# A graph-attention kernel on one core: batch 0's self features as seven block products, and the loads of batch 1 in pieces

## The chip, the core and the metric

The kernel runs on one core of a Trainium2 chip. A core has a matrix engine (TensorE, PE in the profile; its weight loads are listed apart as PEld), three engines for elementwise work (VectorE, DVE; ScalarE, ACT; GpSimd, POOL) and a queue engine (SyncE, SP) that issues nearly all DMAs here. Engines run their own instruction lists in order and wait for each other through semaphores. The metric is the device time of one execution in microseconds (us); lower is better.

## The reference

A graph-attention layer over B = 16 batches of N = 512 nodes with F = 512 features; only the first NG = 20 nodes of a batch are attended to, there are 16 heads of 32, two directions d, and 11 edge labels.

```python
row_zero = v.sum(-1) == 0
q_exp = where(row_zero[..., None], 0.0, q[:, None, :])
self_feat = concatenate([v, q_exp], -1) @ W_self.T + b_self      # (B, N, 512)
output = self_feat
for d in range(2):
    A = (adj if d == 0 else swapaxes(adj, 1, 2))[:, :, :20, :]   # (B, N, 20, 11)
    cond, vb = A.sum(-1), A @ w_bias + b_bias
    kv = self_feat[:, :20]
    aff = where(cond[:, :, None] > 0, q_d(self_feat) . k_d(kv) / sqrt(32), -9e15) + vb[:, :, None]
    output += einsum(softmax(aff) over the 20 nodes, kv, Wout[d]) + bout[d]
return v + relu(output)
```

The part that matters most here is `self_feat`: for each batch a 512 x 512 by 512 x 512 product in fp32, plus a query term where the node's row is not all zero.

## The kernel before

Everything is held with features on the 128 partitions (four chunks of 128) and nodes along the free dimension. There is a setup, and then a loop over 16 batches; each batch has four tiles (`nt` = 0 to 3) of 128 nodes. The order of the instructions on every engine is the order in which the program writes them (`manual_schedule`); nothing reorders them.

**Setup.** Weights are loaded; the features of the 20 attended nodes of all batches (`kvn`, `kvT`) and their keys (`khD`) are computed. Keys are then multiplied by the query weights, so that scores can be taken from `self_feat` directly. This runs in 22 bursts (`keys`): a burst is 16 small matmuls into two PSUM pairs, which ScalarE (L683) and VectorE (L685) empty into the stage tiles `st`; finished stages go out by DMA, to `g0` (batch 0, kept in SBUF), `g1_d` (batch 1) and `g_d` (the others), both in HBM. A burst uses both PSUM pairs, so the next can begin only when both are emptied; between two bursts TensorE does something else, by the list `plan`: one entry per burst from the fifth (n = 4) on, each letter one step. `v` and `w` are the products that make the values (`values`, results to `vw_d` in HBM), `c` the bias scores (`bias_scores`), `n` the flags for rows that are zero (`row_flags`), `s` a sixteenth of a part of batch 0's self features (`self_step`, L205). VectorE adds the query term to a finished part (`self_copy`, L218). POOL, in the same bursts, sums rows (`row_sums`), makes sums and differences of the blocks of W_self (`weight_sums`) and multiplies the masks of batch 0 (`mask_mul`, `mask_count`, `mask_sum`, `mask_spread`).

**Self features.** For batches 1 to 15 the product is done by blocks: x and W_self are cut in two by two blocks, and seven products of 246 columns (`product`, L282) of sums of blocks (`x_sum` on POOL, `weight_sums`) stand for the eight plain ones; `partial` (L289) and `joined` (L299) on VectorE read them out of PSUM and add the query term. The 20 attended nodes are copied from `kvn` (`new_self`). For batch 0 the plain products are used, in four parts `(f, h)` (output half f, node half h): three in the setup, the fourth in batch 0 between the scores of its first and second tile (`self_feat(0, 1, 1)`).

**A tile.** `scores` (L356, 128 matmul records), into one of two PSUM pairs; `weigh` on VectorE adds the masks (`full_add` on POOL makes them from `cq` and the spread masks `both`) and subtracts the maximum; `expo` on ScalarE; one tile later `normal` (sum and reciprocal on VectorE, multiplication on POOL, L411) and `turn` (transpose into `wt`, VectorE). In tile 2 of batch b the attention of batch b - 1 is done (`attend`, L429), from `wt` and the value blocks `vd`; `finish` adds the self features and `residual` adds x.

**Value blocks.** `vd` is read from `bd_d` in HBM (`load_values`), a block-diagonal layout for all batches. In batch 0 `bd_d` is set to zero by one DMA of 2 MB (`clear_blocks`), and then 12 DMAs copy the values of all batches from `vw_d` into it, in runs of 32 numbers (`blocks`).

**SP's queue.** All these loads are issued by SP in program order, and each waits on SP for what it needs; `behind(dma, instruction)` adds a wait for a named instruction, so that loads of steady batches go out one by one. In batch 0 of the kernel before, the keys of batch 1 are loaded in one DMA ahead of the loop, and at the start of tile 1 the masks of batch 1 (`load_adj`), `cq` (`load_cq`), the clear, and the natural rows of batch 2 (`load_xn`, for the zero flags: `row_sum` on ScalarE, `row_mask` on POOL) go out without such waits; the copies stand at the start of tile 2, `load_values(0)` at the start of tile 3.

Of the kernel before, what the change touches and what calls it, by code (L numbers as in the profile page):

```python
# [13 lines left out]
P = 128  # L14
# [4 lines left out]
def gat_kernel(  # L19
# [71 lines left out]
    adds, fulls, wts, outs, held, sf_ps, conds, prods = {}, {}, {}, [], [None] * 3, {}, {}, {}  # L91
    sums, parts, us, done = {}, {}, {}, {}
# [57 lines left out]
    def blocks():  # L150

        bb = bd_d.rearrange("c b r e i g -> (c b) r e i g")
        vv = vw_d.rearrange("d c (b m) (e g) -> d (c b) m e g", m=NG, e=HL)
        for e in range(HL):
            for i in range(2):
                j = (e * S) // 32 + i
                for d in range(2):
                    lo = max(e * S + d * NG, 32 * j)
                    hi = min(e * S + (d + 1) * NG, 32 * j + 32)
                    if lo < hi:  # L160
                        m, r = lo - e * S - d * NG, lo - 32 * j
                        nc.sync.dma_start(bb[:, r : r + hi - lo, e, i], vv[d, :, m : m + hi - lo, e])
# [31 lines left out]
    def self_feat(b, f, h, parts=((0, range(C)), (1, range(C)))):  # L194


        lo, hi = max(NG, h * N // 2), (h + 1) * N // 2
        for i, ks in parts:
            if (i, ks[0]) == (0, 0):
                if (f, h) == (0, 0):  # L200
                    new_self(b)
                held[0] = bank(f"ps_sf{b}_{f}{h}", 3 if (f, h) == (1, 1) else None)
            for k in ks:
                for a in range(HL):
                    nc.tensor.matmul(  # L205
                        held[0][bass.ts(a, R), i * N // 2 : i * N // 2 + hi - lo],
                        ws_v[:, k, bass.ds((2 * f + i) * P + a * R, R)], xs[b][:, k, lo:hi],
                        start=(k == 0), stop=(k == C - 1),
                    )
            if (i, ks[-1]) == (1, C - 1):  # L210
                sf_ps[b, f, h] = held[0]

    def self_copy(b, f, h):

        lo, hi = max(NG, h * N // 2), (h + 1) * N // 2
        ps = sf_ps.pop((b, f, h))
        for i in range(2):
            nc.vector.scalar_tensor_tensor(  # L218
                sfs[b][:, 2 * f + i, lo:hi], nzs[b][:, lo:hi], qw[:, 2 * f + i, b : b + 1],
                ps[:, i * N // 2 : i * N // 2 + hi - lo], ALU.mult, ALU.add,  # L220
            )

# [15 lines left out]
    def x_sum(b, n):  # L238

        t = sums[b, n] = xsum.tile([P, 2, HN], F32, tag=f"t{n}", name=f"t{b}_{n}")  # L240
# [8 lines left out]
    def product(b, n):  # L249
# [11 lines left out]
        if n == 1:  # L261
            parts[b, "a"] = [bank(f"ps_a{b}_{i}", i) for i in range(2)]
        if n == 2:
            parts[b, "d"] = bank(f"ps_d{b}", 2)
        if n == 5:
            parts[b, "c"] = bank(f"ps_c{b}", 3)
# [30 lines left out]
    def joined(b, n, key, f, l):  # L297

        done["joined"] = nc.vector.tensor_add(  # L299
            block(b, f, l), parts[b, key][:, : 2 * HN].rearrange("p (i n) -> p i n", i=2), us.pop((b, n))  # L300
# [30 lines left out]
    def mask_spread(b, h, quarters=range(4)):  # L331

        add = conds[b, h]
        for a in quarters:
            for g in range(HL):
                r = bass.ts(g, R)
                nc.scalar.copy(adds[b, h][bass.ts(a, R), :, g], add[r].rearrange("p (t m) -> p t m", t=2))  # L337
# [29 lines left out]
    def weigh(b, nt, ps, between=None):  # L367

        f = softmax_view(fulls.pop((b, nt)))
        nc.vector.tensor_add(  # L370
# [81 lines left out]
    with tc.tile_pool(name="setup", bufs=1) as sp, tc.tile_pool(name="ps_acc", bufs=4, space=PSUM) as acc["pool"]:  # L452
# [157 lines left out]
        with tc.tile_pool(name="setup_g", bufs=4) as sg:  # L610
# [451 lines left out]
```

## Time and profile before

| | |
|---|---|
| median of 3 runs | 587.73 us (587.0 to 588.74) |
| the profiled execution's own time | 589.14 us |
| its span (first to last instruction) | 587.3 us |
| TensorE busy | 575.0 us (98%) |
| VectorE, ScalarE, POOL busy | 84%, 67%, 65% |
| granted TensorE clock | 0.995 |
| HBM traffic | 82.30 MB read, 40.24 MB written |

The profile's page lists busy times, the chain of work that ended last, the costliest groups of instructions and the DMAs; other views give an engine's instructions in order of time, who waited for whom, and busy times by stretches. In a row of a timeline the first number is the start in us from the span's start, the second the time in us until the last instruction of the row ends; `x32` counts instructions; `a<-b` is output and inputs; a bracket tells how long the engine was idle before and what ended that. Rows with SPq are DMAs being issued, and their time is that of issuing, not of the transfer. One fp32 matmul of the program leaves two matmul records. A busy TensorE is a list of matmuls without gaps; it is not TensorE at its peak.

### The profile page before, as it was taken

To read this page: it belongs to the slowest core of one execution; us is meant where nothing else is said; L and a number is where in the kernel's file an instruction comes from. 1 tells how busy PE (TensorE), PEld (TensorE's weight loads), DVE (VectorE), ACT (ScalarE), POOL (GpSimd) and SP (SyncE) were. 2 spreads that over 40 slices of the span, in tenths; PEclk is the share of its full clock that TensorE was granted. 3 is DMA by queue.
4 is the path that set the end of the run, shared out by engine and by line. 5 is a ranking of instruction groups with operands and counts; after the bars stand their busy time and mean duration, and the time that the engine had idled before them with its cause. 6 is when DMAs were issued, how large, how long until landed. Compare 5 with 4: busy or idle time off the path is not lost.

```text
span 587.3 us, 30302 instructions
## 1 busy us (share of the span) xinstructions
PE 575.0 (98%) x13180; PEld 436.8 (74%) x13180; DVE 491.2 (84%) x785; ACT 395.5 (67%) x1162; POOL 384.3 (65%) x351
## 2 busy tenths in 40 slices
PE   9999999999999999999999999999999999999993
PEld 6654547887778787877778787787878878787881
DVE  1485565889898989899999999998989898989895
ACT  1334534686877777878686868686877868776761
POOL 2406663548677685858586867776868686777774
PEclk9999999999999999999999999999999999999998
DMA  8999899857766675757676767675666766664403
GB/s 312 387 400 314 330 376 333 256 110 209 231 179 188 188 211 169 216 172 214 173 201 180 217 169 210 175 210 167 198 196 188 210 187 182 210 171 136 121 31 127
DMA packets 103221, 124.14 MB, mean 211 GB/s; under 512 B 21713, under 2 KB 71921, under 8 KB 101041
## 3 DMA queue, kind: packets, MB, share of 16 engines
q1 hardware_dynamic: 101840, 120.32, 66.3%
q8 instruction: 104, 1.70, 1.2%
q0 software_dynamic: 672, 1.36, 1.0%
q10 hardware_dynamic: 576, 0.53, 0.3%
q14 instruction: 29, 0.23, 0.1%
HBM read 82.30 MB, written 40.24 MB: 209 GB/s over the span
## 4 chain that ended last, share of the span: by engine, by line
PE 94%; DVE 3%; DMA 1%; issue 1%; ACT 0%; POOL 0%; SPq 0%; DVEq 0%; POOLq 0%; ACTq 0%
PE ps_s L356 44%; PE ps_a L282 17%; PE ps_c L282 9%; PE ps_o L429 6%; PE ps_d L282 4%; PE ps_v L643 3%; PE ps_k L580 3%; PE ps_sf L205 2%; DMA ws_q<-in_wsT 1%; PE ps_kv L531 1%; DVE o L438 0%; PE ps_nz L189 0%; DVE wt L418 0%; DVE ps_s L374 0%; DVE sm L409 0%
## 5 line engine op out<-in xcount | busy, mean ns | idle before, releaser
L356 PEld LDWEIGHTS ps_s<-g,sf 128*32 128x32 f32 x8192 | 263.3, 110 | 20.1 <-issue 12.2
L356 PE MATMUL ps_s<-g,sf 128*32 128x152 f32 x8192 | 276.7, 293 | 0.5 <-ACT st L683 0.5
L337 ACT COPY both<-add 32x80 f32<-32x80 f32 x512 | 130.9, 256 | 53.6 <-DVE add L328 47.6
L411 POOL TENSOR_TENSOR s<-s,sm 128x640 f32<-128x640 f32 x63 | 80.3, 1275 | 95.5 <-DVE sm L410 54.7
L344 POOL TENSOR_TENSOR full<-cq,both 128x640 f32<-128x640 f32 x64 | 100.2, 1565 | 28.5 <-issue 22.6
L317 ACT ACTIVATE prod<-adj,wb_sb 128x80 f32<-128x80 int32 x330 | 112.5, 432 | 0.8 <-DMA adj<-in_adj 0.8
L383 ACT ACTIVATE s<-s 128x640 f32<-128x640 f32 x63 | 46.5, 738 | 65.6 <-DVE s L378 65.3
L443 POOL TENSOR_TENSOR o<-o,x 128x512 f32<-128x512 f32 x60 | 76.0, 1288 | 0.0
L370 DVE TENSOR_TENSOR full<-ps_s,full 128x608 f32<-128x608 f32 x63 | 48.9, 777 | 29.7 <-PE ps_s L356 24.4
L409 DVE TENSOR_REDUCE sm<-s 128x32 f32<-128x640 f32 x63 | 50.9, 807 | 9.2 <-ACT s L383 8.9
L282 PE MATMUL ps_a<-t,ws_s 128*32 128x246 f32 x960 | 55.4, 370 | 0.0
L374 DVE TENSOR_REDUCE ps_s<-full 128x32 f32<-128x640 f32 x63 | 52.2, 828 | 2.2
L418 DVE STREAM_TRANSPOSE wt<-s 128x640 f32<-128x640 f32 x63 | 52.8, 839 | 0.1
L378 DVE TENSOR_TENSOR s<-full,ps_s 128x640 f32<-128x640 f32 x63 | 51.5, 818 | 1.1
L282 PEld LDWEIGHTS ps_a<-t,ws_s 128*32 128x32 f32 x960 | 31.5, 110 | 16.1
L328 DVE TENSOR_REDUCE add<-prod 128x80 f32<-128x960 f32 x32 | 36.8, 1150 | 6.1 <-ACT prod L317 4.3
L247 POOL TENSOR_TENSOR t<-x 128x492 f32<-128x492 f32 x30 | 34.4, 1148 | 10.2 <-DVE full L370 5.3
L429 PE MATMUL ps_o<-wt,vd 32*32 32x512 f32 (+5 forms) x816 | 37.8, 578 | 2.3 <-DVE wt L403 2.0
L440 ACT ACTIVATE o<-o,bo 128x512 f32<-128x512 f32 x60 | 38.3, 711 | 0.6 <-POOL biased L888 0.6
L438 DVE TENSOR_TENSOR o<-ps_o,sf 128x512 f32<-128x512 f32 x60 | 36.7, 668 | 0.0
L289 DVE SCALAR_TENSOR_TENSOR u<-nz,qw,ps_a 128x246 f32<-128x246 f32 x90 | 36.6, 449 | 0.0
L247 POOL TENSOR_TENSOR t<-x,t 128x492 f32<-128x492 f32 x30 | 34.4, 1147 | 1.9 <-DMA x<-in_xT 0.7
(238 smaller groups left out, 719.6 us busy)
## 6 DMA issues: line engine op xcount, KB each, us to landing
g_d<-st SPq DMA_DIRECT2D x16, 1064.0 KB, 5.8
g<-g_d SPq DMA_DIRECT2D x56, 304.0 KB, 3.6
out_T<-o SPq DMA_DIRECT2D x60, 256.0 KB, 3.5
x<-in_xT SPq DMA_DIRECT2D x56, 256.0 KB, 3.3
xn<-in_xn SPq DMA_DIRECT2D x52, 256.0 KB, 3.2
adj<-in_adj SPq DMA_DIRECT2D x56, 220.0 KB, 3.3
nz<-nz_d SPq DMA_DIRECT2D x14, 256.0 KB, 4.3
wk<-in_wkT SPq DMA_DIRECT2D x2, 1024.0 KB, 7.6
```

The costliest lines, as they stand in the source:

```text
L247: done["xsum"] = nc.gpsimd.tensor_sub(t, one, two)
L282: nc.tensor.matmul(to, lhs, x[:, k], start=start, stop=stop, skip_group_check=n != 2)
L317: nc.scalar.activation(p[:, :, l], a[:, :, l], AF.Identity, scale=wb_sb[:, l : l + 1])
L337: nc.scalar.copy(adds[b, h][bass.ts(a, R), :, g], add[r].rearrange("p (t m) -> p t m", t=2))
L344: done["full"] = nc.gpsimd.tensor_add(f, cqs[b].unsqueeze(1).to_broadcast(shape), adds[b, nt // 2][:, nt % 2].unsqueeze(2).to_broadcast(sh ...
L356: nc.tensor.matmul(bank[bass.ts(a, R), bass.ts(j, WD // HL)], sfs[b][:, k, bass.ds(nt * P + (2 * g + j) * R, R)], keys[:, k, a], start=(k ...
L374: nc.vector.tensor_reduce(mx, f, AX.X, ALU.max)
L378: done["weigh"] = nc.vector.tensor_sub(s, f, mx.unsqueeze(3).to_broadcast(full))
L411: done["normal"] = nc.gpsimd.tensor_mul(s, s, sm.unsqueeze(3).to_broadcast(full))
L418: nc.vector.transpose(wts[b][:, nt], s.rearrange("p a h m -> p (a h m)"))
L429: nc.tensor.matmul(banks[a][bass.ds(at // 2 * DH, n * DH)].rearrange("p (t n) -> p t n", n=32), vd[r, bass.ds(at * DH, n * DH)], wt[r, :, ...
L443: nc.gpsimd.tensor_add(o[:, c], o[:, c], xs[b][:, c])
```

## The change

Batch 0 gets its self features by the same seven block products as the others. They are steps `p` of the setup's plan, one per burst, in the last seven bursts; each is followed by its `partial` or `joined` on VectorE. For that `weight_sums` and the row sums of batch 1 move to burst 9, `new_self(0)` and the four block sums of batch 0 to burst 11; the block sums lie in a tile of the pool of the self features. The `v`, `c`, `w` and `n` steps are dealt out anew over the earlier bursts. The fourth part between batch 0's first two tiles of scores goes, with its `self_copy`. In all batches `partial` now writes straight into the self features and `joined` adds in place, without a tile of its own, and `new_self(b + 1)` stands in tile 2 in place of tile 3.

In batch 0 the loads of SP's queue are cut: `bd_d` is cleared in eight DMAs of 256 KB, batch 1's masks go out in four halves, its keys in four pieces, batch 2's natural rows in four pieces. Most wait for a named instruction of batch 0. The first three tiles order them so: two mask halves, clears 0 and 1 (tile 0); clears 2 and 3, `cq`, keys 0, clears 4 to 7 (tile 1); keys 1, two mask halves, and the 12 copies with keys 2 and 3 and the four pieces of natural rows among them (tile 2). Batch 2's x follows; `load_values(0)` moves from tile 3 of batch 0 to tile 0 of batch 1, behind `joined`. `row_sum(2)` on ScalarE moves from tile 3 of batch 0 to tile 0 of batch 1, behind the second mask product, and `row_mask(2)` behind `full_add(1, 1)`.

```diff
-    def clear_blocks(zero):
-        nc.sync.dma_start(
-            bd_d.rearrange("c b r e i g -> (c b r) (e i g)").rearrange("(n p) w -> p n w", p=P),
-            zero.unsqueeze(1).to_broadcast([P, C * B * 32 // P, HL * 2 * DH]),
-        )
+    def clear_blocks(zero, n, ins):
+        half = bd_d[n // 2, n % 2 * (B // 2) : (n % 2 + 1) * (B // 2)]
+        behind(nc.sync.dma_start(
+            half.rearrange("b r e i g -> (b r) (e i g)").rearrange("(n p) w -> p n w", p=P),
+            zero.unsqueeze(1).to_broadcast([P, B * 16 // P, HL * 2 * DH]),
+        ), ins)
...
-                        nc.sync.dma_start(bb[:, r : r + hi - lo, e, i], vv[d, :, m : m + hi - lo, e])
+                        copies.append((bb[:, r : r + hi - lo, e, i], vv[d, :, m : m + hi - lo, e]))
+        for n, (to, of) in enumerate(copies):
+            nc.sync.dma_start(to, of)
+            if n in (2, 5):
+                load_keys(1, range(n // 3 + 2, n // 3 + 3))
+            if n in (7, 8, 9, 10):
+                load_xn(2, (n - 7) // 2, None, slice((n - 7) % 2, (n - 7) % 2 + 1))
...
-    def partial(b, n, f, l, to=None):
-        if to is None:
-            to = us[b, n] = xsum.tile([P, 2, HN], F32, tag=f"u{n}", name=f"u{b}_{n}")
+    def partial(b, f, l):
+        to = block(b, f, l)
...
-            def self_step(b, f, h, i, k):
-                self_feat(b, f, h, ((i, (k,)),))
-                if (i, k) == (1, C - 1):
-                    self_copy(b, f, h)
+            def block_product(n):
+                product(0, n)
+                f, args = {
+                    1: (partial, (0, 0, 0)), 2: (joined, (0, "d", 0, 0)), 6: (partial, (0, 0, 1)),
+                    7: (partial, (0, 1, 1)), 5: (joined, (0, "c", 1, 1)), 4: (partial, (0, 1, 0)),
+                    3: (joined, (0, "c", 0, 1)),
+                }[n]
+                f(*args)
...
+                "p": [(block_product, (n,)) for n in (1, 2, 6, 7, 5, 4, 3)],
...
-            plan = "bvv vv vv ccw vv ns ssss sssw vv vv ssss ssss vv vv nww ssss ssss".split()
+            plan = "bvv vvc vvc vvn vv vvw vv vv w w wn p p p p p p p".split()
...
+                if n == 9:
+                    row_sums(1)
+                    weight_sums()
                 if n == 11:
-                    row_sums(1)
-                if n == 13:
-                    weight_sums()
+                    new_self(0)
+                    for i in range(1, 5):
+                        x_sum(0, i)
...
-        load_keys(1)
...
                 if b == 0 and nt == 1:
-                    load_adj(1, 0)
-                    load_cq(1)
-                    clear_blocks(zero)
-                    load_adj(1, 1)
-                    load_xn(2, 0)
-                    load_xn(2, 1)
-                if b == 0 and nt == 2:
-                    blocks()
-                if nt == 2 and last or nt == 3 and b == 0:
+                    clear_blocks(zero, 2, done["xsum"])
+                if nt == 2 and last:
                     load_values(b)
...
+                        if b == 1:
+                            for j in range(4):
+                                row_sum(2, j)
                         product(b, 4)
...
-                        if b > 1:
-                            load_values(b - 1, done["joined"])
+                        load_values(b - 1, done["joined"])
...
+                    if b == 0:
+                        clear_blocks(zero, 3, done["sum"])
+                        load_cq(1)
...
-                    if b == 0:
-                        self_feat(0, 1, 1)
...
+                    if b == 0:
+                        load_keys(1, range(1), done["mixed"])
+                        clear_blocks(zero, 4, done["normal"])
...
+                    if b == 0:
+                        clear_blocks(zero, 7, done["full"])
...
+                    if b == 0:
+                        load_keys(1, range(1, 2), done["sum"])
+                        load_adj(1, 1, done["normal"], slice(0, 1))
+                        load_adj(1, 1, None, slice(1, 2))
+                        blocks()
```

More of the change, by code (lines that the diff above doesn't have):

```diff
@@ L191, in row_flags @@
         nc.vector.tensor_scalar(nzs[b], ps[:, :N], 0.0, None, ALU.not_equal)
[L194 to L221, printed above, removed]
     def weight_sums():
@@ L912, in gat_kernel @@
                         product(b + 1, 2)
[L913 removed]
+                        new_self(b + 1)
+                    s = weigh(b, nt, pair, (lambda: partial(b + 1, 0, 0)) if more else None)
                     expo(s)
```

65 lines of the change are left out of this document (38 added, 27 removed).

## The prediction, made before the changed kernel was run

> **What bounds the kernel now.** I read the chain that ended last first, then TensorE's waits, then the two places that the diff touches (the bursts at the end of the setup, and SP's queue in batch 0), each on the engines' timelines.
>
> ```profile
> PE 94%; DVE 3%; DMA 1%; issue 1%; ACT 0%; POOL 0%; SPq 0%; DVEq 0%; POOLq 0%; ACTq 0%
> ```
> ```profile
> PE ps_s L356 <- ACT st L683: 0.5, 1, 0.5
> ```
> The first row is the chain that ended last, by engine: TensorE (PE) carries 94% of the span. The second is TensorE's wait ahead of the very first scores; hardly any other wait of its matmuls exists. So whatever shortens TensorE's list of matmuls counts, and whatever makes TensorE wait in batches 0 and 1 counts as much. The matmuls themselves, in the chain in order of time (start, us, what, matmul records):
>
> ```profile
> 58.06 1.73 PE ps_sf L205 x32
> ...
> 85.45 1.86 PE ps_sf L205 x32
> ...
> 91.15 4.34 PE ps_s L356 x128
> 95.49 3.45 PE ps_sf L205 x64
> ...
> 111.41 1.66 PE ps_a L282 x32
> ```
> L205 is batch 0's old self_feat: a half of a group of 236 columns takes 1.73, of 256 columns 1.86; three groups (two of 236, one of 256) are in the setup, the fourth, 3.45, stands between batch 0's first and second scores. The first scores run from 91.15 to 95.49; I call their end E. A block product (L282, 246 columns, 32 records) takes 1.66 in the loop.
>
> Now SP's queue, which issues all DMAs of batch 0 in order (start, us until the last is issued):
>
> ```profile
> 108.46 11.54 SPq L162 DMA_DIRECT2D bd_d<-vw_d  x12
> 124.38 3.12 SPq L139 DMA_DIRECT2D vd<-bd_d  x4
> 127.55 1.84 SPq L105 DMA_DIRECT2D x<-in_xT  x4
> ```
> The 12 copies into the value blocks are issued in 11.54 us, until 120.00. The read of the value blocks (vd, four DMAs) reads what they write, so it starts only at 124.38, 4.4 after the last copy's issue: this is the landing of the last copy. The attention of batch 0, which needs vd, runs on TensorE here:
>
> ```profile
> 132.06 2.24 PE L429 MATMUL ps_o<-wt,vd 32*32 32x512 f32 x48
> 134.23 4.34 PE L356 MATMUL ps_s<-g,sf 128*32 128x152 f32 x128
> 138.39 1.84 PE L282 MATMUL ps_a<-x,ws_v 128*32 128x246 f32 x32
> ```
> It starts at 132.06. How much earlier vd was there is told by its landings:
>
> ```profile
> DMA to landing us min/median/max: 1.7/3.2/3.4
> ```
> The last of the four is issued at about 127.1 (124.38 + 3.12 less its own 0.4) and is down 1.7 later, at 128.8: 4.4 after the first one's issue, and 3.3 before TensorE wanted it. That 3.3 is the room which the change can use up in SP's queue before TensorE stands.
>
> **The change part by part.**
>
> TensorE's work. Removed from the setup: 4 x 1.73 + 2 x 1.86 = 10.6. Added there: seven block products. In the setup a filler between two bursts costs more than the same work in the loop (a half of 256 columns 1.86 there, 3.45 / 2 = 1.73 in the loop), so I put 246 columns between 1.73 and 1.86: 1.80, seven are 12.6. Bounds: 1.66 (11.6) and 1.86 (13.0). Setup: +2.0. Removed from batch 0: -3.45.
>
> Fillers and evictions. Between two bursts of key products TensorE does a filler, and the next burst needs the PSUM pair that ScalarE and VectorE (DVE) empty.
>
> ```profile
> 43.16 1.98 PE L643 MATMUL ps_v<-wo_sb,kvT 128*128 128x512 f32 x4
> ...
> 56.59 0.78 PE L668 MATMUL ps_g(1, 3, 1, 0, 2)0_552<-khD,wq_sb 32*128 32x304 f32 x4
> ...
> 57.99 1.80 PE L205 MATMUL ps_sf<-x,ws_v 128*32 128x236 f32 x32
> 59.72 0.40 PE L668 MATMUL ps_g(2, 0, 0, 1, 2)0_594<-khD,wq_sb 32*128 32x152 f32 x2
> ...
> 60.70 1.40 PE L205 MATMUL ps_sf<-x,ws_v 128*32 128x236 f32 x24
> ...
> 82.53 1.94 PE L643 MATMUL ps_v<-wo_sb,kvT 128*64 128x512 f32 x8
> ```
> ```profile
> 43.32 1.17 DVE L685 TENSOR_SCALAR st<-ps_g(0, 3, 1, 1, 2)1_410 128x304 f32<-128x304 f32 x2 [0.52 <-PE ps_g(0, 3, 1, 1, 2)1_410 L668]
> ...
> 76.99 1.06 DVE L322 TENSOR_REDUCE cond<-adj 128x80 f32<-128x880 int32 x1
> ...
> 109.14 0.84 DVE L289 SCALAR_TENSOR_TENSOR u<-nz,qw,ps_a 128x246 f32<-128x246 f32 x2
> ```
> In the burst before 43.16 the eviction starts 0.16 after the filler and takes 1.17: a filler shorter than 1.33 makes TensorE wait. The new plan has two bursts followed by a lone w step; two w steps together take 1.94 (82.53), so one takes 0.97: two waits of about 0.37. Old waits that go: the burst at 56.59 lasts until 57.99, 1.40, where the one at 59.72 lasts until 60.70, 0.98 (0.42, behind a VectorE that was late), and the 0.5 ahead of the first scores, since a product now stands between the last burst and them. VectorE's new load is two instructions per partial (0.84) and one per join, which I count at 0.84 too: 1.17 + 0.84 = 2.0 in a burst of 0.98 + 1.80 = 2.78, hidden; only where batch 0's second mask count (1.06) joins them, 3.07, does it stick out by 0.3. Sum of waits: 0.74 + 0.3 - 0.92 = +0.1; bounds -0.9 (no new wait) and +2 (0.3 at each of the seven products).
>
> POOL. Row sums, weight sums and four subtractions move ahead. The first product that uses a sum is the third, six bursts behind the subtractions' place; four POOL operations at 1.28 (the row of 640 elements below) are 5.1 against at least 5 x 2.78. Nothing on the path; if POOL were that late, each product would wait for one subtraction.
>
> So the first scores begin at 91.15 + 2.0 + 0.1 = 93.2, E moves from 95.49 to 97.6 (+2.1), and everything behind the old fourth group is 2.1 - 3.45 = -1.4 earlier: attention of batch 0 is due at 130.7.
>
> SP's queue. Clearing the value blocks becomes 8 DMAs instead of 1, batch 1's masks 4 instead of 2, its keys 4 instead of 1, batch 2's natural rows 4 instead of 2; most wait for a named instruction of batch 0, and what is queued behind such a wait waits too. The gates end with the last clear, which waits for the third full_add of batch 0, on POOL:
>
> ```profile
> 103.94 1.57 POOL L344 TENSOR_TENSOR full<-cq,both 128x640 f32<-128x640 f32 x1
> 107.87 1.28 POOL L411 TENSOR_TENSOR s<-s,sm 128x640 f32<-128x640 f32 x1 [2.36 <-DVE sm L410]
> ```
> It ended at 103.94 + 1.57 = 105.5, which is E + 10.0; nothing of it depended on the old fourth group, so with the new E it ends at 107.6, and the last clear goes out there. The first copy waits for that clear to land; 256 KB take
>
> ```profile
> out_T<-o SPq DMA_DIRECT2D x60, 256.0 KB, 3.5
> ```
> 3.5, so copies start at 111.1. Bounds: the two mask halves in front of them wait for the next POOL row (normal, 1.28, till 108.9) and cost two plain issues (0.46, a quarter of the 1.84 for x): not before 109.8; and 114.6 with twice the landing. Among the 12 copies now stand 6 plain DMAs (two of keys, four of rows). I charge 6 x 0.46 = 2.8; lower bound 0 (the copies' queue has room), upper 6 x 0.96 = 5.8 (the copies' own pace). Copies issued by 111.1 + 11.5 + 2.8 = 125.4, landed 4.4 later at 129.8. Batch 2's x, which was behind vd, now goes ahead of it, but in the time of that landing. vd needs 4.4 again: 134.2. TensorE wants it at 130.7 and stands 3.5. Queued behind the attention are the next tile's scores and everything after, so the stall goes into the time in full.
>
> Late next. Keys of batch 1: the third piece is issued after three copies, the fourth after six, about 111.1 + 6 x 0.96 + 0.9 = 117.8, landing (3.5) 121.3. The second half of batch 1's first scores is due, counted back from 132.06 by a tile of scores (4.3), a product (1.7) and half a tile (2.2), at 123.9, less 1.4: 122.5. Hidden, by 1.2; if that cover is gone, TensorE stands here first and the attention's stall is as much shorter. Row sums of batch 2 on ScalarE now stand behind the second mask product and wait for rows that are issued among the last copies:
>
> ```profile
> 121.14 3.77 ACT L317 ACTIVATE prod<-adj,wb_sb 128x80 f32<-128x80 int32 x11
> 126.20 2.13 ACT L337 COPY both<-add 32x80 f32<-32x80 f32 x8 [1.29 <-DVE add L328]
> 129.00 0.74 ACT L383 ACTIVATE s<-s 128x640 f32<-128x640 f32 x1 [0.66 <-DVE s L378]
> ```
> The mask product (121.14, 3.77) ends at 123.5 in the new time. The fourth rows are the 17th of 18 issues, about 124.0, landing 127.5; a row sum (taken as the 0.74 of the exponential) ends 128.2, half a mask spread 2.13 later, so the exponential due at 127.6 starts at 130.3: 2.7 late. Its readers on VectorE feed the product at 138.39, so it costs between 0 and 2.7 by itself, and nothing while attention stands for 3.5 anyway. Writing partials straight into self_feat, joining in place, and the copy of the first 20 columns one tile earlier change no count of instructions in batches 1 to 15: nothing.
>
> Sum. +2.0 + 0.1 - 3.45 + 3.5 = +2.1. The profiled execution took 589.14 (span 587.3), 1.4 above the median 587.73: 591.2 on its scale, 589.8 on the median's.
>
> [...] How loaded the DMA engines were is in the view by stretches (us; busy time of PE, PEld, DVE, ACT, POOL; clock; DMA share, GB/s):
>
> ```profile
> 103.00:107.00 4.00, 4.00 (x132) 4.00 (x128) 3.68 (x5) 1.26 (x3) 2.51 (x2) 1.00 1.08 377
> 123.00:127.00 4.00, 4.00 (x123) 3.80 (x119) 3.47 (x5) 2.68 (x9) 3.25 (x4) 1.00 0.13 24
> ```
> vd's 1.7 landing falls into the quiet stretch (share 0.13), while the clear's stretch before had a share of 1.08. [...]
>
> **Rivals.**
> Landings are short, and vd is in time. In the quiet stretch a DMA landed in 1.7. With 1.7 for the last clear the copies start at their gate, 109.8; issued by 124.1, landed 125.8, vd there at 130.2, just before 130.7. Then -1.4 stays: 586.3; with products at 1.66 up to another 1.0 less. It decides at a vd that lands 3.5 sooner than I charge. For it: the queue is no longer filled at once. Against it: the last copy of before took 4.4, most of it in a stretch in which SP issued nothing else; x's two extra DMAs now fall into it.
> The queue is fuller. The rows and keys among the copies (6 x 0.96) and a slow clear (114.6): vd at 114.6 + 11.5 + 5.8 + 4.4 + 4.4 = 140.7, ten late: 596. With half of it, 593. For it: share 1.08 whenever large loads stood together before; against: with a share of 0.13 at 123 to 127 the engines had time to spare while SP waited for the last copy.
> The setup does not take seven products. VectorE's two instructions per product could set the pace of the last seven bursts: 0.3 each, +2 more: 592.
>
> **How the numbers follow.** A measurement of this kernel tells 0.3% (1.8 us) from no change. Forecast 0.42 (589.8, own range 588 to 592; about a third of it within 0.3%), short landings 0.30 (two thirds of it faster by over 0.3%, since the open ends of the products' and the waits' terms, 1.0 each, lie below its -1.4; the rest within), fuller queue 0.20, setup 0.08. Faster 0.20, same 0.25, slower 0.55. The range goes from 585.3 (short landings with cheap products) to 594.5 (half to three quarters of the fuller queue).
>
> **What the changed profile would show.** Right: in the setup 32-record products of about 1.8; first scores starting near 93.2; no L205; in SP's queue copies starting near 111 and vd issued near 130; a TensorE wait of some 3.5 ahead of the attention of batch 0, put down to vd. Wrong: the attention starting right behind scores near 130.7, or a wait at another place: keys of batch 1, row sums on ScalarE.

## The result, and the profile after

The changed kernel takes 591.14 us (median of 7 runs, 590.69 to 595.46) against 587.16 for the kernel before (7 runs, 586.28 to 588.74): a ratio of 1.0082, 95% interval 1.0065 to 1.0099. It is slower by 0.8%.

The chain that ended last, by engine, and TensorE's waits, of the changed kernel:

```profile
PE 88%; DVE 3%; SPq 3%; DMA 2%; issue 1%; POOL 1%; ACT 1%; DVEq 0%; POOLq 0%; ACTq 0%
```
```profile
PE ps_o L413 <- DMA vd<-bd_d: 4.9, 1, 4.9
```

TensorE's share of the chain fell from 94% to 88%; SP's queue (SPq) and DMAs, which were next to nothing, have 5%. The waits name the place: 4.9 in front of batch 0's attention (L413), for vd. The wait of 0.5 ahead of the first scores, which the prediction showed, is gone. The chain in order of time shows both parts of the change (start, us, what):

```profile
74.73 1.80 PE ps_a L267 x32
...
91.13 1.80 PE ps_c L267 x32
92.93 1.80 PE ps_s L340 x55
...
107.70 3.90 DMA bd_d<-zero
...
121.67 1.93 SPq L111
...
125.47 2.16 SPq L111
...
127.67 3.43 DMA bd_d<-vw_d
...
131.19 4.38 DMA vd<-bd_d
...
135.70 4.00 PE ps_o L413 x48
```

The seven products of the setup take 1.80 each, and the first scores start at 92.93. From 107.70 on the chain leaves TensorE: the last clear lands 3.90 after its issue, then come SP's issues, among them two rows of batch 2 (L111) at 1.93 and 2.16, the last copy lands 3.43 after its issue at 127.67, and the first piece of vd 4.38 after 131.19. TensorE's own timeline around it (start, us, engine, line, what; in brackets the idle time before):

```profile
126.30 4.46 PE L340 MATMUL ps_s<-g,sf 128*32 128x152 f32 x128
135.70 4.00 PE L413 MATMUL ps_o<-wt,vd 32*32 32x512 f32 x48 [4.94 <-DMA vd<-bd_d]
139.63 4.34 PE L340 MATMUL ps_s<-g,sf 128*32 128x152 f32 x128
...
167.93 2.24 PE L413 MATMUL ps_o<-wt,vd 32*32 32x512 f32 x48
```

The scores ahead of the attention end at 126.30 + 4.46 = 130.76. TensorE then stands 4.94, and the 48 records of the attention, 2.24 in the kernel before, take 4.00. The stretches between show why (us; busy time of PE, PEld, DVE, ACT, POOL; granted clock; DMA share, GB/s):

```profile
131.00:135.70 4.70, 0.00 (x0) 0.03 (x1) 1.98 (x4) 4.50 (x16) 1.93 (x3) 1.00 0.85 254
135.70:139.70 4.00, 4.00 (x52) 1.16 (x56) 2.24 (x3) 1.76 (x5) 4.00 (x4) 0.58 0.69 108
139.70:142.00 2.30, 2.30 (x76) 2.30 (x80) 2.22 (x4) 2.30 (x8) 0.38 (x1) 1.00 0.70 214
```

The granted clock is 0.58 in the 4 us after the wait, and 1.00 before and after. At full clock the attention would have ended 4.00 - 2.17 = 1.83 sooner (2.17 by the chain of a later experiment). The next scores start at 139.63 instead of 134.23, 5.4 later: -1.4 from the work that is gone, + 4.94 + 1.83. ScalarE and VectorE were late as well:

```profile
130.12 0.63 ACT L177 ACTIVATE xn<-xn 128x512 f32<-128x512 f32 x1 [0.49 <-DMA xn<-in_xn]
...
132.88 0.74 ACT L367 ACTIVATE s<-s 128x640 f32<-128x640 f32 x1
```
```profile
133.65 0.82 DVE L393 TENSOR_REDUCE sm<-s 128x32 f32<-128x640 f32 x1 [4.16 <-ACT s L367]
...
139.78 2.48 DVE L422 TENSOR_TENSOR o<-ps_o,sf 128x512 f32<-128x512 f32 x4 [1.80 <-PE ps_o L413]
```

The four row sums of batch 2 (L177) wait for their rows from 124.5 to 130.1, so the exponential behind them starts at 132.88 (it had been due at 127.6), and VectorE waits 4.16 for it. VectorE still stands 1.80 for the attention at 139.78: this lateness is covered by the stall.

One attention later, in batch 1, the two kernels stand 4.43 apart (167.93 above, and this row of the kernel before):

```profile
163.50 2.24 PE L429 MATMUL ps_o<-wt,vd 32*32 32x512 f32 x48
```

Between its two attentions the kernel before needed 31.44 (163.50 - 132.06), where a batch otherwise takes 30.48: its profiled execution lost 1.0 there, 1.5 in later batches and 1.2 behind the last attention. So the two profiled executions end only 1.7 apart (590.85 and 589.14), while the medians are 4.0 apart. In these two executions nothing more is lost once batch 1 attends; how much of the kernel before's own losses its other executions have is not shown, since only one has a profile.

### The profile page after: what moved, and what is told of

It reads as the page before. It is cut to its first block, busy times and chain, and to the rows that moved or that the text cites. A ratio compares the mean times of both kernels' runs of the same rounds, so it can differ in the third digit from the quotient of the medians.

```text
span 589.1 us, 30279 instructions
## 1 busy us (share of the span) xinstructions
PE 574.8 (98%) x13148; PEld 437.3 (74%) x13148; DVE 493.1 (84%) x788; ACT 395.5 (67%) x1162; POOL 388.6 (66%) x355
## 4 chain that ended last, share of the span: by engine, by line
PE 88%; DVE 3%; SPq 3%; DMA 2%; issue 1%; POOL 1%; ACT 1%; DVEq 0%; POOLq 0%; ACTq 0%
PE ps_s L340 40%; PE ps_a L267 17%; PE ps_c L267 9%; PE ps_o L413 6%; PE ps_d L267 4%; PE ps_k L564 3%; PE ps_v L627 3%; PE ps_kv L515 2%; SPq L166 1%; SPq L111 1%; DMA vd<-bd_d 1%; DMA bd_d<-zero 1%; DMA bd_d<-vw_d 1%; PE ps_warm L474 1%; POOL s L395 0%
## 5 line engine op out<-in xcount | busy, mean ns | idle before, releaser
L267 PE MATMUL ps_a<-t,ws_s 128*32 128x246 f32 x1024 | 59.4, 371 | 0.6 <-issue 0.6
L273 DVE SCALAR_TENSOR_TENSOR sf<-nz,qw,ps_a 128x246 f32<-128x246 f32 x128 | 51.6, 443 | 0.7 <-PE ps_a L267 0.7
L267 PEld LDWEIGHTS ps_a<-t,ws_s 128*32 128x32 f32 x1024 | 33.4, 110 | 18.5 <-POOL s L395 1.0
L413 PE MATMUL ps_o<-wt,vd 32*32 32x512 f32 (+5 forms) x816 | 38.6, 609 | 7.2 <-DMA vd<-bd_d 4.9
L232 POOL TENSOR_TENSOR t<-x 128x492 f32<-128x492 f32 x32 | 36.8, 1149 | 9.5 <-DVE full L354 6.9
L232 POOL TENSOR_TENSOR t<-x,t 128x492 f32<-128x492 f32 x32 | 36.7, 1146 | 1.3
```

What stands on the lines that cost most here:

```text
L232: done["xsum"] = nc.gpsimd.tensor_sub(t, one, two)
L267: nc.tensor.matmul(to, lhs, x[:, k], start=start, stop=stop, skip_group_check=n != 2)
L273: done["partial"] = nc.vector.scalar_tensor_tensor(to[:, i], nzs[b][:, half(l)], qw[:, 2 * f + i, b : b + 1], parts[b, "a"][i][:, :HN], AL ...
L413: nc.tensor.matmul(banks[a][bass.ds(at // 2 * DH, n * DH)].rearrange("p (t n) -> p t n", n=32), vd[r, bass.ds(at * DH, n * DH)], wt[r, :, ...
```

## The experiments

Theory A: the change pays for SP's queue. The copies start late behind gated clears and have other DMAs among them, so vd is late, and the clock falls behind the wait. Theory B: it pays for row sums that hold up ScalarE. Theory C: it pays in the setup. Every ratio is against the kernel before on the same chip in the same session, with a 95% interval. The last column is the ratio times 587.16 us; the expected times are to be held against it, since they start from the chip on which the kernel before took 587.16. (The 587.1 that e7 and e8 name for e1 is its own median, with 588.04 for the kernel before beside it.)

| kernel | ratio | interval | us at 587.16 |
|---|---|---|---|
| changed kernel | 1.0082 | 1.0065 to 1.0099 | 591.14 |
| e1 block products alone | 0.9983 | 0.9969 to 0.9998 | 586.2 |
| e2 loads alone | 1.0073 | 1.0051 to 1.0096 | 591.4 |
| e3 ten matmuls in the wait | 1.0139 | 1.0118 to 1.0160 | 595.3 |
| e12 five matmuls in the wait | 1.0085 | 1.0063 to 1.0107 | 592.2 |
| e4 scores ahead of the attention | 1.0058 | 1.0035 to 1.0082 | 590.6 |
| e5 rows early | 1.0040 | 1.0026 to 1.0054 | 589.5 |
| e6 no named waits | 0.9987 | 0.9966 to 1.0009 | 586.4 |
| e7 block products, rows behind the copies | 0.9999 | 0.9989 to 1.0008 | 587.1 |
| e11 no named waits, vd ahead of x, late row sums | 0.9997 | 0.9979 to 1.0015 | 587.0 |
| e8 block products, clear ahead of keys | 0.9997 | 0.9985 to 1.0009 | 587.0 |
| e9 block products, clear in the setup | 1.0011 | 0.9998 to 1.0023 | 587.8 |
| e10 the same, other loads spread | 1.0041 | 1.0020 to 1.0063 | 589.6 |

**e1, e2: the two halves of the change.** e1 keeps the new products and puts every load back; e2 keeps the old self_feat and takes every new load.

```diff
 e1 (against the changed kernel)
+        load_keys(1)
                 if b == 0 and nt == 1:
-                    clear_blocks(zero, 2, done["xsum"])
+                    load_adj(1, 0)
+                    load_cq(1)
+                    clear_blocks(zero)
+                    load_adj(1, 1)
+                    load_xn(2, 0)
+                    load_xn(2, 1)
+                if b == 0 and nt == 2:
+                    blocks()
...
 e2 (against the kernel before): the same lines the other way round
```

> Only the block products of the change; keys, masks, rows, clear, copies and the read of the value blocks in the order of before. If the queue of the loads is what the change pays for (theory A): the setup's +2.1 less the fourth group's 3.45 stays alone, 1.4 under the kernel before, 585.8 (585.0 to 586.5), and no wait of TensorE ahead of batch 0's attention. If the setup pays (theory C: products or evictions there cost more than the chain of waits shows): 587 to 589. If ScalarE's row sums pay (theory B): 585.8 as well, since they are back at their old place.

> Only the loads of the change; self_feat of batch 0 by the four old groups. The gates hang on batch 0's first scores, which are 2.1 earlier than in the changed kernel, so vd is down near 135.7 - 2.1 = 133.6, while attention is due at 132.06 as before. Theory A: a stall of 1.5, and between 0 and 1.8 for an attention that runs slowly behind it: 588.7 to 590.5. Theory C: no change, 587.2. Theory B: ScalarE's exponential of batch 1's first tile is as late behind its due time as in the changed kernel, but less is hidden by the shorter stall: up to 592.

The loads alone carry the whole loss: 1.0073, as much as the changed kernel within the intervals. The products alone are 0.17% faster, about 1.0 of the 1.4 us expected, by an interval that just leaves out no change. C falls: 586.2 lies in A's range. e2's 591.4 lies above A's range and under B's 592, and its trace decides: TensorE waits for vd, and in the products behind the attention there is no wait for VectorE. In e2 the attention stalls and runs slowly as in the changed kernel (TensorE's timeline):

```profile
135.65 3.99 PE L437 MATMUL ps_o<-wt,vd 32*32 32x512 f32 x48 [3.33 <-DMA vd<-bd_d]
```

The stall is 3.33, not 1.5: the copies start at 111.7 there, hardly earlier than in the changed kernel, and the attention takes 3.99 again. In e1's profile no wait for vd is left, but TensorE has two waits in batch 0, of 1.9 and 0.7, with no releaser: nothing that the profile shows ended them, and it calls them `issue`. During the longer one the DMA engines' share was 1.07. This profiled execution took 588.66, the longest of e1's twelve:

```profile
PE ps_s L335 <- issue: 1.9, 1, 1.9
```
```profile
104.00:108.00 4.00, 2.08 (x67) 1.75 (x63) 3.31 (x5) 2.55 (x7) 4.00 (x4) 1.00 1.07 371
```

**e6: the named waits.** Every `done[...]` of the clears, of batch 1's masks and of its first two keys becomes None; the order of the queue stays.

```diff
-                    clear_blocks(zero, 2, done["xsum"])
+                    clear_blocks(zero, 2, None)
...
-                        load_adj(1, 1, done["normal"], slice(0, 1))
+                        load_adj(1, 1, None, slice(0, 1))
```

> The changed kernel without the named waits of the eight clears, of batch 1's masks and of its first two keys; the order of the queue is the same, rows and keys stay among the copies. Theory A: the copies start by 105 instead of 111.8, vd is down before attention is due (130.8), the wait of 4.9 and the slow attention go: 584.3 to 586, unless loads at a full queue cost something else. Theory B: rows land as much earlier, so this one alone does not tell the two apart. If the pace of the copies and not their start sets vd (their issue is 16.4 long): vd moves by less, 587 to 589.

0.9987 instead of 1.0082: the named waits are what the change pays for. The copies start 3.1 earlier than in the changed kernel (108.66, not the 105 that was expected: SP still waits 2.3 for the clears to land), and vd goes out 3.3 earlier (127.92 instead of 131.19). The time, 586.4, lies 0.4 above A's range (SP's queue, vd's landings, TensorE):

```profile
108.66 2.29 SPq L166 DMA_DIRECT2D bd_d<-vw_d  x3
...
127.92 1.72 SPq L139 DMA_DIRECT2D vd<-bd_d  x4
```
```profile
DMA to landing us min/median/max: 3.6/4.0/4.4
```
```profile
132.44 2.72 PE L413 MATMUL ps_o<-wt,vd 32*32 32x512 f32 x48 [1.81 <-DVE full L354]
```

The first vd is down at 127.92 + 4.4 = 132.3, 0.1 before the attention starts; the releaser that the row names, an addition on VectorE, is not read by the attention. Idle for 1.81, TensorE kept its clock (1.00 from 128 to 136): the attention takes 2.72 in place of 4.00. What it takes above 2.17 may be the wait for vd's other pieces; that is not shown.

**e5: the rows out of the copies.**

```diff
                     clear_blocks(zero, 2, done["xsum"])
+                    load_xn(2, 0)
+                    load_xn(2, 1)
...
-            if n in (7, 8, 9, 10):
-                load_xn(2, (n - 7) // 2, None, slice((n - 7) % 2, (n - 7) % 2 + 1))
```

> The changed kernel with batch 2's natural rows loaded in two DMAs behind the third clear, as early as before, instead of in four among the copies; the two keys stay among the copies, all named waits stay. Theory A (SP's queue): without the four row issues (5.3 us of SP's time in the changed kernel) the copies are issued by 124, landed by 128, vd is bound by its own named wait and down near 131 to 132.5: a stall of 0.3 to 1.7 in place of 4.9, and an attention of 2.2 to 3: 585.5 to 588. Theory B (row sums on ScalarE): the row sums no longer wait, exponential and adds are on time; the attention still waits for vd 4.9 if the rows did not hold vd up: 589 to 591.

Neither. The time, 589.5, lies in B's range, but the wait that B named, 4.9 for vd, is not there. The rows, 1 MB ahead of the last clears, held those up in the queue, and the copies started 3.8 later than in the changed kernel. Now the keys, which go between the copies, were late before vd was (SP's queue, TensorE's timeline):

```profile
107.52 5.53 SPq L146 DMA_DIRECT2D bd_d<-zero  x4
...
115.61 3.82 SPq L166 DMA_DIRECT2D bd_d<-vw_d  x3
```
```profile
127.49 3.14 PE L338 MATMUL ps_s<-g,sf 128*32 128x152 f32 x56 [2.47 <-DMA g<-g_d]
```

TensorE waited 2.5 and 1.5 for keys, its clock fell to 0.57 at that place (128 to 132), and with so much time lost vd was ready. The wait moved in front of another instruction, as theory A's queue would have it, but the 585.5 to 588 was wrong: what goes ahead of the clears delays the copies too. The loss is half that of the changed kernel, 1.0040.

**e3, e12: work in the wait.**

```diff
+                        if b == 1:
+                            for n in range(10):          # e12: 5
+                                nc.tensor.matmul(banks[n % 4], ws_v[:, 0, :P], xs[1][:, 0], start=True, stop=True)
                         attend(b - 1, banks)
```

> The changed kernel with ten matmuls of 512 columns (about 0.5 us each) in front of batch 0's attention, into the PSUM banks that the attention then overwrites; their results are not used. They stand where TensorE waited 4.9 us. If the attention took 4.00 instead of 2.17 because the granted clock falls behind an idle TensorE (0.58 in that stretch): it takes 2.2 again and the time is 591.1 - 1.8 = 589.3. If it is slow for another reason (weights that have just landed, PSUM, DMA traffic): 4.0 as before and 591.1. In both cases the start of the attention stays near 135.7.

> The changed kernel with five instead of ten of the extra matmuls in front of batch 0's attention; the ten took 8.78 (0.88 each, not the 0.5 that was reckoned with), so five take 4.4 and end half a microsecond before vd is down. The start of the attention stays near 135.7. If the slow attention costs its 1.8 in full: the attention takes 2.2 and the time is 1.8 under the changed kernel, 1.0051 of before. If ScalarE's late exponential and VectorE behind it would have held the next products up anyway (theory B, up to 2.1 in the other kernels): the attention takes 2.2, but TensorE waits later for VectorE and the time stays at 1.0082. If the clock is not it: attention 4.0, 1.0082.

The attention behind work takes 2.17 and 2.24, not 4.00 (chain in order of time of e3; timeline of e12), into the same PSUM banks and with the DMA engines' share at 0.59 in e12 (140 to 144; 0.69 in the changed kernel): its slowness came from the wait in front of it, not from PSUM or traffic. Nor from a vd that has just landed: in e4, below, the attention starts right behind vd's landing and runs at a clock of 1.00 (122 to 152).

```profile
133.66 8.78 PE ps_o L897 x20
142.44 2.17 PE ps_o L413 x48
```
```profile
126.28 3.66 PE L340 MATMUL ps_s<-g,sf 128*32 128x152 f32 x56 [1.99 <-DVE add L312]
...
135.69 4.56 PE L897 MATMUL ps_o<-x,ws_v 128*128 128x512 f32 x10
140.18 2.24 PE L413 MATMUL ps_o<-wt,vd 32*32 32x512 f32 x48
```

The times do not price it, and the attention starts at 142.44 and 140.18, not near 135.7. The ten matmuls took 8.78, longer than the wait they filled; in both runs the keys were late, so that TensorE waited in batch 1's first tile (1.76 in e3, 1.99 in e12). In e12 the scores behind ran slowly (3.66, against 2.02 in e4 below), and the extra matmuls began at 135.69 instead of 130.76. The row blames a sum on VectorE, which the scores don't read; the last key piece, issued at 120.3, landed 5.8 later, at 126.1:

```profile
DMA to landing us min/median/max: 3.5/4.7/5.8
```

**e4: the wait filled with the next scores.**

```diff
+                    if b == 1:
+                        for g in range(2):
+                            scores(b, nt, g, ps[g])
                     if b > 0:
                         banks = [bank(f"ps_o{b - 1}_{q}", q) for q in range(4)]
                         attend(b - 1, banks)
...
-                    for g in range(2):
+                    for g in range(2 if b != 1 else 0):
                         scores(b, nt, g, ps[g])
```

> The changed kernel with batch 1's third tile of scores (4.3 us) ahead of batch 0's attention instead of behind it, nothing else. Theory A: the scores fill the wait of 4.9 but for 0.6, and the clock stays at 1.0: 591.1 - 4.3 - 1.8 = 585.0. Theory B (ScalarE's late exponential would have held TensorE up by itself, the wait for vd only hid it): the wait moves to the next product or scores and only a part comes back: 587.7 to 590.

```profile
124.36 2.02 PE L340 MATMUL ps_s<-g,sf 128*32 128x152 f32 x56 [1.28 <-DMA g<-g_d]
...
136.45 2.90 PE L413 MATMUL ps_o<-wt,vd 32*32 32x512 f32 x48 [0.15 <-DMA vd<-bd_d]
140.15 1.87 PE L267 MATMUL ps_a<-x,ws_v 128*32 128x246 f32 x32 [0.79 <-DVE o L422]
...
145.02 1.87 PE L267 MATMUL ps_a<-t,ws_s 128*32 128x246 f32 x32 [1.35 <-DVE sf L273]
```

The wait for vd shrinks to 0.15, but waits of 0.79 and 1.35 for VectorE come up ahead of the first and the third product behind the attention, and one of 1.28 for keys in batch 1's first tile. So in the trace only a part came back, as theory B had it, and a little less than its 590 (590.6): three waits were lined up, and the longest had covered the others. The time alone does not show it: 1.0058 and the changed kernel's 1.0082 have intervals that overlap.

**e7, e11: the price of late row sums.** e7 is e1 with batch 2's rows behind the copies and the row sums where the change has them. e11 is e6 with the rows behind the copies, vd next, and the row sums behind the whole mask spread.

```diff
 e7 (against e1)
-                    load_xn(2, 0); load_xn(2, 1)
                 if b == 0 and nt == 2:
                     blocks()
+                    for n in range(4):
+                        load_xn(2, n // 2, None, slice(n % 2, n % 2 + 1))
...
                         mask_mul(b, 1)
+                        if b == 1:
+                            for j in range(4):
+                                row_sum(2, j)
```

> The block products alone (loads as before), but batch 2's rows issued behind the copies and their row sums on ScalarE in batch 1's first tile behind the second mask product, as in the changed kernel. The rows fall into the landing of the last copy, so vd is at most 1 later than with the block products alone. Theory B: ScalarE's exponential of batch 1's first tile is about as late as in the changed kernel (row sums end near 130) without a wait for vd to hide it; what it costs by itself, 0 to 2.7, stands above the block products alone (587.1): 587.1 to 590. Theory A: nothing of it reaches TensorE: 586 to 587.5.

> The changed kernel without the named waits of the clears, masks and first keys, and with batch 2's rows behind all copies, the read of the value blocks right behind these (ahead of batch 2's x), and the row sums on ScalarE behind the second half of the mask spread instead of ahead of the first. Both suspected costs are taken away at once: copies issued by 120, vd down by 128 to 129 and attention due near 130.7 (theory A), no exponential that waits for rows (theory B: the 2.1 that the block products with late row sums showed ahead of batch 2's products go too). Left are TensorE's waits without releaser, 1.0 to 2.0 in the kernels that load without named waits: 0.9960 to 0.9980 of before. If one of the two theories misses a cost, TensorE waits for vd, keys, nz or a product's partial and the time is that of the changed kernel without named waits (0.9987) or above.

Without a stall for vd to cover it, e7 shows theory B's cost (TensorE's waits): 1.3 + 0.8 = 2.1, the same two waits as in e4. Its wait without releaser is shorter than e1's, 1.0. By the times e7 is some 0.16% above e1, measured in another session and with intervals that overlap.

```profile
PE ps_a L262 <- DVE sf L268: 1.3, 1, 1.3
...
PE ps_s L335 <- issue: 1.0, 1, 1.0
PE ps_a L262 <- DVE o L417: 0.8, 1, 0.8
```

In e11 TensorE did not wait for vd, and the two waits stayed (timelines of TensorE and VectorE):

```profile
130.70 2.42 PE L411 MATMUL ps_o<-wt,vd 32*32 32x512 f32 x48
...
137.81 1.87 PE L265 MATMUL ps_a<-x,ws_v 128*32 128x246 f32 x32 [0.43 <-DVE o L420]
...
142.69 1.87 PE L265 MATMUL ps_a<-t,ws_s 128*32 128x246 f32 x32 [1.35 <-DVE sf L271]
```
```profile
136.34 0.85 DVE L400 STREAM_TRANSPOSE wt<-s 128x640 f32<-128x640 f32 x1 [2.96 <-POOL s L393]
```

ScalarE was on time, but the row mask made from the sums sits in POOL's queue ahead of a normalisation, and VectorE stood 2.96 for that one. Moving the row sums moved the wait from ScalarE to POOL. By the times it gains nothing over e6: 0.9997.

**e8, e9, e10: can the loads be better placed?** All three have the products and the loads of e1, but: in e8 the 2 MB clear goes ahead of batch 1's keys; in e9 it goes out in eight pieces between the setup's bursts; e10 is e9 with keys, masks and rows in pieces behind named instructions.

```diff
 e8                                   e9
+        clear_blocks(zero)           +                if 3 < n < 12:
         load_keys(1)                 +                    clear_blocks(zero, n - 4)
```

> The block products alone, with the one clear of 2 MB issued ahead of batch 1's keys at the end of the setup instead of behind them. It can go out some 3 us before the keys, which wait for the setup's last store. If TensorE's waits of 1.9 and 0.7 that have no releaser (in the block products alone, while the DMA engines' share was above 1.0) come from the full DMA engines, an earlier start spreads the same bytes: 584.5 to 586.5 against 587.1; if they do not: 587.

> The block products alone, with the clear of 2 MB in eight pieces issued between the setup's bursts (from the fifth on) instead of in batch 0; the other loads in the order of before. If TensorE's waits without releaser in batch 0 (1.0 to 2.0 in the three kernels that load at a share above 1.0 there) come from the full DMA engines, two of the five MB leave that stretch and the waits shrink below 1: 0.9970 of before (585.4 to 586). The copies no longer wait for the clear, so vd is no later than 128. If the waits have another cause: 0.9983 as the block products alone. If the pieces delay the setup's stores of keys: 1.000 or more, with waits in the setup.

> The same with the clear in the setup, and batch 1's keys and masks and batch 2's rows in pieces behind named instructions of batch 0, as the change has them, but all issued ahead of the copies' end and with vd read as in the kernel before. Theory A: spreading by itself costs nothing once vd (down by 129) is not behind it: no wait at the attention, no wait without releaser above 0.7, no late row sums: 0.9960 to 0.9970 of before. If pieces and gates are what costs: 1.002 or more, with a wait for vd or keys.

None beats e1. In e8 TensorE waited 1.99 with no releaser, and the scores behind ran at a clock of 0.67:

```profile
102.92 7.90 PE L335 MATMUL ps_s<-g,sf 128*32 128x152 f32 x185 [1.99 <-issue]
```
```profile
104.00:108.00 4.00, 4.00 (x92) 4.00 (x88) 1.24 (x2) 0.28 (x2) 4.00 (x4) 0.67 1.08 329
```

In e9 the pieces delayed the setup's own stores of keys: one that went out at 77.32 landed 6.99 later (chain), and TensorE stood 1.7 behind ScalarE, which waited for that store's buffer, a wait that e1 does not have: the third of the outcomes that had been named. A wait with no releaser stays. It is 1.0 long, and it is 1.0 in e7 too, where the 2 MB clear was still there, so that the clear's bytes set its length is not shown:

```profile
77.32 6.99 DMA g_d<-st
```
```profile
PE ps_g(3, 1, 1, 0, 2)0_820 L648 <- ACT st L663: 1.7, 1, 1.7
...
PE ps_s L336 <- issue: 1.0, 1, 1.0
```

e10 has the same wait in the setup (1.9) and one without releaser of 1.8, during which the share was 0.33, so it does not need full DMA engines:

```profile
PE ps_s L336 <- issue: 1.8, 1, 1.8
```

## Why the prediction was right

The change was forecast at +2.1 us and measured at +4.0 (the forecast's 589.8 stands on a median of 587.73 for the kernel before, the measured 591.14 on 587.16). The likeliest case was the one that happened, at the place named, by the mechanism named: gates, late copies, a late vd, a stall in front of batch 0's attention. That the total is no further off is in part luck, as the terms show.

- **Products at 1.80, first scores near 93.2:** 1.80 and 92.93. The two bursts behind a lone w step lasted 1.30 and 1.39 instead of 0.98, the few tenths that were counted. The attention was due at 130.7: 130.76.
- **Removing the fourth group with nothing else worth -1.4:** e1 gives -0.17% (-1.0, by its interval -1.8 to -0.1). Its profile has waits without releaser, which were no term of the sum.
- **The gates end near 107.6, copies start at 111.1:** 107.70, and 111.78, since the clear took 3.90 to land instead of 3.5. e6, which takes the gates away, shows that this term carries the loss.
- **Copies issued by 125.4 (mis-sized):** 128.2. The copies themselves took less than the 11.5 charged; the four row issues, charged at 0.46, took 0.60, 1.93, 0.62 and 2.16. The last copy's landing, counted from the end of the issues as in the forecast, took 2.9 instead of 4.4 (128.2 to 131.1) and gave 1.5 back.
- **vd's 4.4, met by luck:** the forecast counted from the first piece's issue until the last piece was down, with landings of 1.7 to 3.4. Here TensorE started when the first piece was down, which alone took 4.38; the last, issued at 132.8 with at least 3.3 to land, can't have been there before 136.1. So the stall of 3.5 came out as 4.94.
- **The attention's own time (missing):** it was taken as 2.2 whatever stood before it. It took 4.00 at a clock of 0.58. With it the loss at this place is 6.8 instead of 3.5 and the sum +5.4, which is how far the next scores stand apart. The medians show 4.0; the kernel before's own losses (1.0 in batch 1 of its profiled execution), which the sum did not count, can make up the rest.
- **Row sums: an exponential 2.7 late, hidden while the attention stands:** it was 5.3 late and hidden. Uncovered, TensorE's waits in e7, e4 and e11 put it at about 2, within the 0 to 2.7 given.
- **Keys hidden by 1.2:** they were, in the changed kernel's profile; in e3, e4, e5 and e12 they were not. That cover was as thin as stated.
- **The rival of short landings** needed vd 3.5 sooner. In the changed kernel the pieces of vd took 3.3 to 4.4 with a DMA share of 0.85 in that stretch, against 1.7 to 3.4 before. The quiet stretch was not there: batch 2's x had been issued right ahead of vd (128.31 to 130.64), while the stretch from 123 to 127, in which vd went out before, had a share of 0.13.

## What to carry to other kernels

A gate that keeps a transfer out of a busy stretch moves everything behind it in the same queue (without the waits, in e6, the copies started 3.1 and vd 3.3 earlier): follow the chain from the last gate to the last reader and compare it with the time that the reader is due, not with the length of the transfers. When a wait goes, look for the next one that was lined up under it before counting the gain: here keys (1.3 in e4) and row sums (2.1 in e4 and e7) lay under vd's 4.9. And a stall of TensorE can cost more than its length: where it was followed by half the clock, as the 4.94 of the changed kernel was (0.50 from 135.65 to 139.06), another 1.7 us went over the next 3.4.

## What was not expected of the hardware

**The clock after a wait.** Waits of 4.94 (the changed kernel), 3.33 (e2), 2.47 (e5), 1.99 (e8, e12), 1.92 (e10, in the setup) and 1.71 (e9) were followed by matmuls that ran slowly: the 56 records of scores that take 2.02 in e4 take 3.14 in e5 and 3.66 in e12, the attention 4.00 instead of 2.17, a product of e9 3.43 where the next ones take 1.80. In the changed kernel the slow stretch has a granted clock of 0.50 and lasts 3.41 us (135.65 to 139.06), so it costs 1.7. The mean clocks of e5 (0.57 from 128 to 132), e8 (0.90 and 0.67 from 100 to 108), e9 (0.79 and 0.79 from 84 to 92) and e10 (0.70 and 0.87 from 84 to 92) give the same as an estimate, about 3.4 each if it is 0.50 there too, whatever the length of the wait. After 1.92 in e1, 1.81 in e6, 1.78 in e10, 1.76 in e3 and 1.28 in e4 the clock stayed at 1.00.

What the traces show beside the length is where the waits fall. The kernel before and the changed kernel also fall to a clock of 0.50 near their end (at 581.64 and 582.80), and in the changed kernel that is 131 times the 3.413 us of its slow stretch after this began at 135.65. Cut into steps of that length, e9's wait fills half of the step ahead of its slow one. e1's longer wait lies across an edge, 0.95 on one side and 0.97 on the other; that the edge is there is an estimate: e1's mean clock of 0.994 over 586.6 us, with nothing else slow on its page, puts its last fall at 579.0 to 580.2, and 139 steps after 105.68 is 580.1 (e9, then e1: us; busy time of PE, PEld, DVE, ACT, POOL; granted clock; DMA share, GB/s):

```profile
82.89:86.31 3.42, 1.71 (x28) 1.12 (x20) 1.55 (x3) 0.75 (x2) 0.46 (x2) 1.00 0.96 380
86.31:89.72 3.41, 3.41 (x34) 1.38 (x32) 1.74 (x3) 1.07 (x2) 1.85 (x2) 0.50 1.02 404
```
```profile
102.26:105.68 3.42, 2.47 (x79) 2.16 (x67) 3.32 (x6) 1.86 (x8) 2.48 (x3) 1.00 1.09 352
105.68:109.09 3.41, 2.44 (x69) 2.40 (x73) 1.87 (x4) 3.41 (x11) 3.41 (x3) 1.00 1.09 383
```

Cut back in the same way from the fall at the end, from 9 us on, the traces of the kernel before and of the changed kernel have three steps that were followed by half the clock, with 2.45 in the one and 3.41 and 1.97 in the other of idle time of TensorE, and no other step ahead of that fall with more than 1.52. With e9's 1.71, that is all that is shown of how much idle time it takes.

**Waits without a releaser.** TensorE stood 0.5 to 2.0 with nothing to wait for in the profile, in e1, e6, e7, e8, e9, e10 and e11, at one or two places in batch 0; the changed kernel and e2, e3, e4, e5 and e12, which keep its spread loads and gates, had at most 0.8 at a place, the kernel before 0.6 and 0.7. Whether they explain how far e1's runs lie apart (585.23 to 588.66) is not shown, since one execution of it has a profile. They stand at regular places of TensorE's list: in e1 and e7 behind 327 of the 384 records of batch 0's first three tiles of scores, in e6, e8 and e11 behind 199, which is 128 earlier, and e1's second one 125 behind its first. What ended them no run shows, and the cause stays open.
